# Sparse graph attention with a feed-forward part: records of the second part by GpSimd's queue, mean factors some steps later, gathers asked four groups ahead

## The chip, the cores and the metric

The kernel runs on one core of one Trainium2 chip. The metric is the device time of one launch in microseconds (us), taken as the median of several runs. The core has five engines with a queue each: TensorE (PE in the profile, with its weight loads as PEld), VectorE (DVE), ScalarE (ACT), GpSimd (POOL) and SyncE (SP). An engine works through its queue in order; an instruction that waits holds up all that stand behind it on the same engine. SP, ACT and POOL also issue DMA transfers.

## The reference

The kernel computes one layer of a graph network on 4096 nodes with 512 features and 8 heads of 64:

```python
hs = layer_norm(x);  ht = layer_norm(h_target)
q = (ht @ Wq + bq) / sqrt(64);  k = hs @ Wk + bk;  v = hs @ Wv + bv     # 8 heads
logits = where(adj != 0, q . k, -1e30)          # 4096 x 4096 per head
ctx = softmax(logits) @ v
ht = layer_norm(ht + ctx @ Wo + bo)
ref = ht + gelu(ht @ W1) @ W2                   # 512 -> 2048 -> 512
out = layernorm(x + ref)
```

`adj` is sparse: a random symmetric matrix with a diagonal of ones, so that a target has some 17 neighbours on average and the largest has several tens. All data are float32.

## The kernel before, in words

The kernel does not form the 4096 x 4096 logits. It turns the adjacency matrix into lists of neighbours and gathers the rows of keys and values that each target needs.

**First stage (0 to about 340 us).** It normalises x, computes keys and values (`project`, L882 and on) and writes them to a table `kvd` in DRAM, one row of 1024 numbers per source. At the same time it reads `adj` and extracts the neighbour lists (`edges`) of the first 16 tiles of 128 targets. `sort(0)` orders these targets by their number of neighbours and scatters one record per target (number, target, factors of its first norm, neighbours) into a DRAM array. The lists of the other 16 tiles are built while the second stage already runs, and `sort(1)` scatters their records (L871) at some 800 us. So there are two parts with 16 tiles each, and a tile has 11 to 39 neighbour slots.

**Second stage, attention.** Tiles are taken in an order that pairs long and short ones; pairs are the groups for the feed-forward part. The slots of a tile are worked off in slot groups of three. For each slot, GpSimd issues an indirect DMA (`gather`, L985) that fetches a key and value row for each of the 128 targets into a slot of the ring `kv`. The ring has 17 slots in the first part and 20 in the second. For a slot group VectorE multiplies keys with the query (L1242), reduces to logits (L1247), and, after ScalarE's exponential, multiplies values with the weights (L1203) and adds two of the slots (L1207). ScalarE does the third slot's values (L1226). PE then adds the slots by transposing them into one PSUM tile (`cps`, L1214), after which the ring slots are free. The attention is a Python generator that yields twice per slot group, that is once per half group.

**Records.** `prefetch(i)` (L989 to L999) loads the record of a tile with a small DMA (128 rows of 116 bytes) two tiles before use; six buffers hold them. In the first part GpSimd issues this load, in the second SP.

**Asking for gathers.** `request(k)` (L1060 to L1070) issues the gathers of all slot groups up to `k + ahead`. `ahead` is `AHEAD` = 4, and 5 once slot group k belongs to the second part.

**Finishing a tile.** `finish` (L1097 to L1168) is a generator that is advanced once per half group (`advance`). It scales the context, projects it with Wo, adds the residual into `h`, takes the moments (L697, L698) and, for the last tile of a group, adds EPS (`shifted`, L680), has GpSimd raise it to -0.5 (`power`, L687), multiplies mean and factor on VectorE (`negmean`, L692), lets ScalarE normalise `h` (L1153), and lets PE transpose it to `h2T` (L1162, copied at L1166). The feed-forward part of the group can begin only then.

**Feed-forward.** `feed(g)` takes `h2T` through hidden matmuls (L1347), ScalarE's GELU (L1350) and output matmuls (L1356), in chunks between which it yields. Halfway it has GpSimd gather the rows of x for its targets into `xt`, of which there are two buffers. After its last chunk the generator `end` (L1298 to L1329) adds x (L1303), takes moments, calls `power`, multiplies the mean factor (L1317), normalises on ScalarE (L1320), and has GpSimd scatter the rows to the output (L1324). `end` is advanced once per chunk of the following group.

**What sets the order.** `_weave` interleaves attention, feed-forward, the remaining lists and late weight loads by costs that each generator yields. That gives a program order; a scheduler of the tile framework then orders each engine's queue anew by its own estimates, with program order as the priority. So a step moved in the source shifts instructions on all engines.

Of the kernel before, what the change touches and what calls it, by code (L numbers as in the profile page):

```python
# [17 lines left out]
P = 128  # L18
# [360 lines left out]
RW = E0 + RE  # L379
# [64 lines left out]
def adj_resnorm_kernel(  # L444
# [33 lines left out]
    nc = tc.nc  # L478
# [34 lines left out]
    recs_d = [dram.tile([n * P, RW], I32, name=f"rec{i}") for i, (_, n) in enumerate(PARTS)]  # L513
# [19 lines left out]
    with tc.tile_pool(name="keep", bufs=1) as keep:  # L533
# [17 lines left out]
        with ExitStack() as late:  # L551
# [131 lines left out]
            def power(pool, mv, n, name, ve=None):  # L683
                if ve is None:
                    ve = shifted(pool, mv, n, name)
                rs = pool.tile([P, n], F32, name=name + "_rs")
                nc.gpsimd.tensor_tensor(rs, ve, mhalf[:, :n], ALU.pow)  # L687
                return rs
# [193 lines left out]
            def project(order, t=None):  # L882
# [81 lines left out]
                for n in range(2, 4):  # L964
                    request(n)
# [23 lines left out]
            def prefetch(i):  # L989
                if i >= NT or i in recs:  # L990
                    return
                r0 = TILES[i][0]
                part = 1 if r0 >= PARTS[1][0] * P else 0
                assert part in done
                r0 -= PARTS[part][0] * P
                rec = sp.tile([P, E0 + MAXE], I32, name="rec", bufs=6)

                (nc.sync if part else nc.gpsimd).dma_start(rec[:, :RW], recs_d[part][r0:r0 + P, :])
                recs[i] = rec  # L999

            def front(i, idle=0):
# [28 lines left out]
                for kc in range(KC):  # L1030
# [11 lines left out]
            SG = [(i, j0, min(S, cap - j0)) for i, (_, cap) in enumerate(TILES)  # L1042
                  for j0 in range(0, cap, S)]
# [8 lines left out]
            first_b = next(k for k, (i, _, _) in enumerate(SG) if i >= NA)  # L1052
            issued = [0]
# [6 lines left out]
            def request(k):  # L1060


                ahead = AHEAD + (1 if k >= first_b else 0)
                while issued[0] <= min(k + ahead, len(SG) - 1):
                    issue(issued[0])
                    mine = set(range(place[issued[0]], place[issued[0]] + SG[issued[0]][2]))
                    for m in range(k, issued[0]):
                        assert not mine & set(range(place[m], place[m] + SG[m][2]))
                    issued[0] += 1
# [27 lines left out]
            def finish(i, p, cps, group, hs, mv):  # L1097


                rec, tq, cap = recs[i], tqs.pop(i), TILES[i][1]  # L1100

                nc.vector.scalar_tensor_tensor(p[:, :cap, :], rec[:, E0:E0 + cap].unsqueeze(2)
                                               .to_broadcast([P, cap, H]), 0.0, p[:, :cap, :],
                                               op0=ALU.is_gt, op1=ALU.mult)
                nc.vector.tensor_reduce(sums[:, i, :], p[:, :cap, :].rearrange("p j h -> p h j"),
                                        AX.X, ALU.add)
                ri = sp.tile([P, H], F32, name="ri")
                nc.vector.tensor_scalar_max(ri, sums[:, i, :], SUM_LO)
                nc.vector.reciprocal(ri, ri)
                rx = sp.tile([P, KC, P], F32, name="rb", bufs=1)  # L1110
                rxf = rx.rearrange("p c t -> p (c t)")
                nc.scalar.copy(rxf.rearrange("p (h d) -> p h d", h=H),
                               ri.unsqueeze(2).to_broadcast([P, H, HD]))
                yield
                yield
                prx = ps.tile([P, KC, P], F32, name="t", bufs=2)
                for c in range(KC):
                    nc.tensor.transpose(prx[:, c, :], rxf[:, c * P:(c + 1) * P], ident)
                ct = sp.tile([P, KC, P], F32, name="rb", bufs=1)
                nc.scalar.copy(ct, prx)  # L1120
                yield
                yield
                nc.vector.tensor_mul(ct, cps, ct)
                yield
                yield
                yield
                yield
                pa = ps.tile([P, D], F32, name="t", bufs=2)

                for c in range(KC):  # L1130
                    nc.tensor.matmul(pa[:, c * P:(c + 1) * P], tq[:, D + c * P:D + (c + 1) * P],
                                     ident, is_transpose=True, start=c == 0, stop=False,
                                     skip_group_check=True)
                for c in range(KC):
                    nc.tensor.matmul(pa, ct[:, c, :], wo[:, c, :], start=False,  # L1135
                                     stop=c == KC - 1, skip_group_check=True)
                turned.add(i)
                yield
                h = sp.tile([P, D], F32, name="h")
                nc.scalar.copy(h, pa)  # L1140
                yield
                stats(sp, h, mv[:, len(hs), :], "n2")
                hs.append(h)
                if len(hs) < len(group):
                    return
                nh = len(hs)
                ve = shifted(sp, mv[:, :nh, :], nh, "n2")
                yield
                rs = power(sp, mv[:, :nh, :], nh, "n2", ve)
                yield  # L1150
                nm = negmean(sp, mv[:, :nh, :], rs, nh, "n2")
                for j, h in enumerate(hs):
                    nc.scalar.activation(h, h, AF.Identity, bias=nm[:, j:j + 1], scale=rs[:, j:j + 1])  # L1153
                yield
                yield
                w = len(hs) * P
                h2T = sp.tile([P, KC, 2 * P], F32, name="h2T")
                for k2 in range(KC // 2):
                    pt = ps.tile([P, 2, 2 * P], F32, name="t", bufs=2)
                    for k in range(2):  # L1160
                        for j, h in enumerate(hs):
                            nc.tensor.transpose(pt[:, k, j * P:(j + 1) * P],  # L1162
                                                h[:, (k2 * 2 + k) * P:(k2 * 2 + k + 1) * P], ident)
                    for k in range(2):
                        kc = k2 * 2 + k
                        nc.scalar.activation(h2T[:, kc, :w], pt[:, k, :w], AF.Identity,  # L1166
                                             bias=b2c[:, kc:kc + 1], scale=s2c[:, kc:kc + 1])
                h2Ts[GROUPS.index(group)] = h2T  # L1168
# [129 lines left out]
            def end(group, xs, po):  # L1298

                nt = len(group)  # L1300
                sm = sp.tile([P, 2, 2], F32, name="sm3")
                for j in range(nt):
                    nc.vector.scalar_tensor_tensor(xs[j], xs[j], 1.0, po[j], op0=ALU.mult,  # L1303
                                                   op1=ALU.add, accum_out=sm[:, j, 0:1])
                nc.vector.tensor_scalar_mul(sm[:, :nt, 0], sm[:, :nt, 0], -1.0 / D)
                yield
                for j in range(nt):
                    nc.scalar.activation(po[j], xs[j], AF.Square, bias=sm[:, j, 0:1],
                                         accum_out=sm[:, j, 1:2])
                yield  # L1310
                ve = sp.tile([P, nt], F32, name="n3_ve")
                nc.vector.tensor_scalar(ve, sm[:, :nt, 1], 1.0 / D, EPS, op0=ALU.mult, op1=ALU.add)
                yield
                rs = power(sp, None, nt, "n3", ve)
                yield
                nm = sp.tile([P, nt], F32, name="n3_nm")
                nc.vector.tensor_mul(nm, sm[:, :nt, 0], rs)  # L1317
                yield
                for j in range(nt):
                    nc.scalar.activation(xs[j], xs[j], AF.Identity, bias=nm[:, j:j + 1],  # L1320
                                         scale=rs[:, j:j + 1])
                yield
                for j, i in enumerate(group):
                    ins = nc.gpsimd.indirect_dma_start(  # L1324
                        out=out[:, :], out_offset=bass.IndirectOffsetOnAxis(
                            ap=tags[:, i, TGT:TGT + 1], axis=0),
                        in_=xs[j], in_offset=None)

                    tc.declare_no_dep(ins.ins, group="out", reason="other rows")  # L1329
                    tc.add_to_no_dep_group("out", ins.ins)  # L1330
# [73 lines left out]
            AHEAD = 4  # L1404
# [112 lines left out]
```

## Time and profile before

| what | us |
|---|---|
| median of 3 runs (lowest, highest) | 1804.25 (1801.67, 1813.1) |
| the profiled execution: its own time | 1802.71 |
| its span | 1800.9 |
| PE busy | 1657.8 |
| DVE busy | 1434.2 |
| ACT busy | 1235.6 |
| POOL busy | 1035.2 |

The page gives busy time by engine, groups of instructions by line, engine and tile with the mean duration of one, and the idle time in front of them with the releaser that ended it. Matmuls are pipelined and a matmul of the program can be two records in the trace. An "issue" behind an arrow is time in which the engine waited for nothing that the profile shows. Windows are in us from the start of the span, and the granted clock of TensorE is a share of full speed.

### The profile page before, as it was taken

To read this page: it belongs to the slowest core of one execution; us is meant where nothing else is said; L and a number is where in the kernel's file an instruction comes from. 1 tells how busy PE (TensorE), PEld (TensorE's weight loads), DVE (VectorE), ACT (ScalarE), POOL (GpSimd) and SP (SyncE) were. 2 spreads that over 40 slices of the span, in tenths; PEclk is the share of its full clock that TensorE was granted. 3 is DMA by queue.
4 is the path that set the end of the run, shared out by engine and by line. 5 is a ranking of instruction groups with operands and counts; after the bars stand their busy time and mean duration, and the time that the engine had idled before them with its cause. 6 is when DMAs were issued, how large, how long until landed. Compare 5 with 4: busy or idle time off the path is not lost. (4 is left out here: it accounts for less than half of the span.)

```text
span 1800.9 us, 22314 instructions
## 1 busy us (share of the span) xinstructions
PE 1657.8 (92%) x6746; PEld 1074.4 (60%) x6746; DVE 1434.2 (80%) x2475; ACT 1235.6 (69%) x3129; POOL 1035.2 (57%) x818
## 2 busy tenths in 40 slices
PE   7999995698999999897899989979999999999995
PEld 3444443566666677565566656656666666666663
DVE  6887786889788879988888989789989798998100
ACT  5876663578687967686677877677878587886210
POOL 1000145757555566788777888778777767782100
PEclk9999998799999999998999999989999999999998
DMA  9999978979878787777888888777787767782000
GB/s 350 373 379 361 346 245 306 362 245 317 275 267 284 266 299 256 256 223 221 310 272 267 290 282 270 262 236 259 247 267 245 250 232 235 256 280 95 24 1 26
DMA packets 142058, 460.99 MB, mean 256 GB/s; under 512 B 18548, under 2 KB 23496, under 8 KB 141928
## 3 DMA queue, kind: packets, MB, share of 16 engines
q0 software_dynamic: 96144, 342.27, 56.6%
q1 hardware_dynamic: 37968, 94.12, 14.9%
q10 hardware_dynamic: 7816, 23.08, 3.2%
q8 instruction: 56, 0.92, 0.2%
q14 instruction: 74, 0.61, 0.1%
HBM read 430.61 MB, written 28.79 MB: 255 GB/s over the span
## 5 line engine op out<-in xcount | busy, mean ns | idle before, releaser
L985 POOL DMA_INDIRECT kv<-kvd,rec x603 | 804.5, 1334 | 336.4 <-PE cps L1214 122.5
L1356 PE MATMUL po<-w,gt 128*128 128x512 f32 x1024 | 469.6, 599 | 0.4 <-ACT gt L1350 0.4
L1347 PE MATMUL pf<-h2T,w 128*128 128x256 f32 (+1 forms) x2176 | 467.0, 368 | 0.2 <-ACT h2T L1166 0.2
L1347 PEld LDWEIGHTS pf<-h2T,w 128*128 128x128 f32 x2176 | 389.2, 191 | 68.4 <-issue 23.2
L1226 ACT ACTIVATE kv<-kv,pa 128x64 f32<-128x64 f32 x1520 | 392.1, 337 | 4.8
L1242 DVE TENSOR_TENSOR kv<-kv,tq 128x1536 f32<-128x1536 f32 (+2 forms) x211 | 352.3, 1677 | 48.0 <-DMA kv<-kvd,rec 35.5
L1247 DVE TENSOR_REDUCE lg<-kv 128x24 f32<-128x1536 f32 (+2 forms) x211 | 351.0, 1667 | 0.5
L1214 PE MATMUL cps<-ident,kv 128*128 128x128 f32 x1724 | 241.1, 287 | 76.4 <-DVE kv L1207 38.9
L1356 PEld LDWEIGHTS po<-w,gt 128*128 128x128 f32 x1024 | 189.4, 193 | 191.9 <-issue 189.7
L1214 PEld LDWEIGHTS cps<-ident,kv 128*128 128x128 f32 x1724 | 213.3, 148 | 150.4 <-DVE kv L1207 50.2
L1203 DVE TENSOR_TENSOR kv<-kv,p 128x1024 f32<-128x1024 f32 (+1 forms) x211 | 251.4, 1193 | 10.9 <-ACT p L1251 9.6
L687 POOL TENSOR_TENSOR n_rs<-n_ve,mhalf 128x2 f32<-128x2 f32 (+2 forms) x51 | 51.4, 1007 | 327.5 <-DVE n_ve L680 148.6
L733 ACT ACTIVATE kv<-kv 128x1024 uint8<-128x1024 int32 x128 | 134.4, 1052 | 53.0 <-DMA kv<-in_adj_dram 24.9
L1350 ACT ACT_TABLE_LOAD x108 | 138.6, 1283 | 1.9
L1350 ACT ACTIVATE gt<-pf 128x512 f32<-128x512 f32 x128 | 76.4, 597 | 87.4 <-PE pf L1347 81.8
L947 PE MATMUL pq<-wk,h2T 128*128 128x512 f32 x256 | 121.6, 618 | 4.3 <-ACT kv L949 2.1
L947 PE MATMUL pq<-wv,h2T 128*128 128x512 f32 x256 | 115.6, 594 | 5.8 <-DVE rbc L662 3.2
L1031 PE MATMUL t<-wq,tq 128*128 128x512 f32 x256 | 117.9, 602 | 0.7 <-ACT tq L1024 0.7
L1135 PE MATMUL t<-wo,rb 128*128 128x512 f32 x256 | 115.5, 592 | 0.0
L742 DVE MAX8 cand<-kv 128x8 uint16<-128x171 uint16 (+1 forms) x384 | 108.4, 325 | 6.5 <-remote 3.7
L1251 ACT ACT_TABLE_LOAD x81 | 103.9, 1283 | 1.5
L1207 DVE TENSOR_TENSOR kv<-kv 128x512 f32<-128x512 f32 x144 | 98.2, 682 | 0.2
(163 smaller groups left out, 1501.4 us busy)
## 6 DMA issues: line engine op xcount, KB each, us to landing
kv<-in_adj_dram SPq DMA_DIRECT2D x128, 512.0 KB
kvd<-tq ACTq DMA_DIRECT2D x23, 512.0 KB
kv<-kvd,rec POOLq DMA_INDIRECT x603
kv<-in_L_gnn_h_target_dram SPq DMA_DIRECT2D x32, 256.0 KB
kv<-in_x_dram SPq DMA_DIRECT2D x15, 512.0 KB
kvd<-kv ACTq DMA_DIRECT2D x9, 512.0 KB
w<-in_L_gnn_W_dram SPq DMA_DIRECT2D x4, 1024.0 KB
w<-in_L_gnn_W_dram ACTq DMA_DIRECT2D x4, 1024.0 KB
```

What stands on the lines that cost most here:

```text
L733: nc.scalar.activation(sg, a, AF.Sign, accum_out=dpart[:, i, h:h + 1])
L947: nc.tensor.matmul(pkv, hT[:, kc, j * P:(j + 1) * P], w[:, kc, :], start=kc == 0, stop=kc == KC - 1)
L985: issues[:] = [nc.gpsimd.indirect_dma_start(out=dst, out_offset=None, in_=table[:, :], in_offset=bass.IndirectOffsetOnAxis(ap=idx, axis=0) ...
L1031: nc.tensor.matmul(pq, hT[:, kc, :], wq[:, kc, :], start=kc == 0, stop=kc == KC - 1)
L1203: nc.vector.tensor_tensor(v4, v4, p[:, j0:j0 + m, :].unsqueeze(3) .to_broadcast([P, m, H, HD]), ALU.mult)
L1214: nc.tensor.matmul(cps[:, c, :], kv[:, j, D + c * P:D + (c + 1) * P], ident, is_transpose=True, start=j0 + j == 0 and c == 0, stop=j0 + n ...
L1226: newest[:] = [nc.scalar.mul(v, v, pa[:, hd:hd + 1]).ins]
L1242: nc.vector.tensor_tensor(kv[:, :n, :D], kv[:, :n, :D], tq[:, :D].unsqueeze(1).to_broadcast([P, n, D]), ALU.mult)
L1247: logits[:] = [nc.vector.tensor_reduce(lg[:, :n, :], kv[:, :n, :D].rearrange("p j (h d) -> p j h d", h=H), AX.X, ALU.add).ins]
L1347: nc.tensor.matmul(pf[:, k, :], w1[(f0 + k) // KC][:, kc, (f0 + k) % KC * P:((f0 + k) % KC + 1) * P], h2T[:, kc, :w], start=kc == 0, stop= ...
L1350: nc.scalar.activation(gt, pf, AF.Gelu_apprx_tanh)
L1356: nc.tensor.matmul(po[j], gt[:, k, j * P:(j + 1) * P], w2[(f0 + k) // KC][:, (f0 + k) % KC, :], start=False, stop=f0 + k == FC - 1, skip_g ...
```

## The change

Four edits:

1. All records are loaded by GpSimd's queue, those of the second part too.
2. `request` asks four slot groups ahead in both parts.
3. In `finish`, four steps instead of one lie between the power and the mean factor, so that L692 and the normalisation of `h` behind it come three half groups later in program order.
4. In `end`, one more step lies between the power and the mean factor of the last norm.

```diff
-                (nc.sync if part else nc.gpsimd).dma_start(rec[:, :RW], recs_d[part][r0:r0 + P, :])
+                nc.gpsimd.dma_start(rec[:, :RW], recs_d[part][r0:r0 + P, :])
...
-                ahead = AHEAD + (1 if k >= first_b else 0)
-                while issued[0] <= min(k + ahead, len(SG) - 1):
+                while issued[0] <= min(k + AHEAD, len(SG) - 1):
...
                 rs = power(sp, mv[:, :nh, :], nh, "n2", ve)
-                yield
+                for _ in range(4):
+                    yield
                 nm = negmean(sp, mv[:, :nh, :], rs, nh, "n2")
...
                 rs = power(sp, None, nt, "n3", ve)
                 yield
+                yield
                 nm = sp.tile([P, nt], F32, name="n3_nm")
```

## The prediction

> **What bounds the kernel now.** I read the page first, then the busy time by stage, then the waits of the second stage by engine, then the two places with the longest stalls in order of time.
>
> ```profile
> PE 1657.8 (92%) x6746; PEld 1074.4 (60%) x6746; DVE 1434.2 (80%) x2475; ACT 1235.6 (69%) x3129; POOL 1035.2 (57%) x818
> ```
>
> TensorE is busy for 1657.8 of 1800.9 us and its work is the same in both kernels, so the time can only move with the 143 us in which PE stands still, and with the time in which it runs at half clock after standing still. The stages say where that is (columns: window, length, busy of PE, PEld, DVE, ACT, POOL, granted clock, DMA share, GB/s):
>
> ```profile
> 0.00:340.00 340.00, 286.58 (x803) 141.71 (x804) 261.33 (x908) 209.42 (x430) 85.39 (x97) 0.94 0.94 342
> 340.00:440.00 100.00, 85.74 (x453) 63.40 (x452) 89.12 (x135) 75.53 (x209) 67.79 (x54) 0.93 0.81 287
> 440.00:700.00 260.00, 258.46 (x1177) 179.32 (x1176) 219.45 (x383) 206.40 (x519) 152.96 (x130) 1.00 0.82 279
> 700.00:1210.00 510.00, 462.49 (x1970) 313.01 (x1969) 447.33 (x518) 373.29 (x1023) 396.59 (x297) 0.95 0.79 261
> 1210.00:1650.00 440.00, 435.47 (x1812) 290.75 (x1811) 393.96 (x450) 337.51 (x882) 321.19 (x231) 1.00 0.74 246
> 1650.00:1801.00 151.00, 129.03 (x539) 86.22 (x537) 23.04 (x85) 33.41 (x70) 11.30 (x13) 0.94 0.05 15
> ```
>
> Up to 340 us lies the first stage, which the change doesn't touch. From 440 to 700 and from 1210 to 1650 PE is full. From 700 to 1210 it stands still for 47.5 us. From 1650 on the attention is over and PE works off what is left of the feed-forward part, alone. In 340 to 440 VectorE is at 89 of 100 us and sets the pace.
>
> Who makes PE stand still between 700 and 1650, and what VectorE waits for (engine, instruction, releaser: us, times, longest), in the answers on waits for PE and for DVE:
>
> ```profile
> PE cps L1214 <- DVE kv L1207: 38.9, 12, 11.0
> PE t L1162 <- ACT h L1153: 6.3, 1, 6.3
> ```
> ```profile
> DVE n_nm L692 <- POOL n_rs L687: 36.1, 6, 14.1
> DVE n_nm L692 <- issue: 20.7, 3, 10.8
> DVE n_nm L1317 <- POOL n_rs L687: 8.8, 5, 3.0
> DVE kv L1242 <- DMA kv<-kvd,rec: 8.8, 5, 2.9
> ```
>
> So VectorE loses 56.8 us in front of `negmean` (L692), waiting for GpSimd's power L687, and 8.8 us for gathers. The worst case, in order of time, VectorE and then GpSimd:
>
> ```profile
> 1158.03 0.16 DVE L680 TENSOR_SCALAR n_ve<-mv 128x2 f32<-128x2 f32 x1
> 1158.11 1.75 DVE L1242 TENSOR_TENSOR kv<-kv,tq 128x1536 f32<-128x1536 f32 x1
> 1173.93 0.16 DVE L692 SCALAR_TENSOR_TENSOR n_nm<-mv,n_rs 128x2 f32<-128x2 f32 x1 [14.08 <-POOL n_rs L687]
> ```
> ```profile
> 1163.45 1.01 POOL L1324 DMA_INDIRECT out_dram<-xt,tags  x1 [0.30 <-issue]
> ...
> 1169.70 0.95 POOL L985 DMA_INDIRECT xt<-in_x_dram,tags  x1 [2.71 <-DMA out_dram<-xt,tags]
> ...
> 1173.17 0.73 POOL L687 TENSOR_TENSOR n_rs<-n_ve,mhalf 128x2 f32<-128x2 f32 x1
> ```
>
> The power's input is ready at 1158.2, but GpSimd's queue still has gathers, a scatter of results and an x gather ahead of it, and reaches it 15 us later. VectorE has one multiply (1.75 us) between, then stands for 14.08 us; PE runs dry 8.5 us behind it.
>
> **The change part by part.** The scheduler deals the instructions out again, so I compare the order in which they stand on each engine in the two built programs.
>
> *Mean factor three half groups later.* Nothing is added; L692 moves. What counts is how much VectorE work stands between L680 and L692. For the five stalls between 850 and 1262 us I add up the instructions there, at the durations of their groups on the page (multiply 1.75, reduce 1.74, values 1.22, half add 0.68). Before: 1.9, 3.8, 6.8, 1.9, 1.4 us. After: 5.6, 8.0, 10.9, 8.1, 4.5 us. The power came 6.5, 8.2, 12.7, 15.7 and 3.9 us after L680; with the same lag the stalls of 5.39, 4.85, 6.59, 14.08 and 2.84 us (sum 33.8) leave about 0.9, 0.2, 1.8, 7.6 and 0, and as two or three fewer gathers stand before the power in the fourth and fifth (398 against 400, 436 against 439), 1.3 us each, some 8 us in all: VectorE gets back 26 us. The four later stalls (7.15, 10.77, 4.54 and 0.62 us) keep nearly all of theirs, since there only 0.5 to 2.1 us stand between even after. PE was full around those, so they cost little either way.
> What reaches PE: its gaps right behind the first four stalls are 0.5, 3.0, 6.3 and 8.5 us, 18.3 in all. I let 4 stand (behind the rest of the fourth), so 14 us are gained. Around the two longest the granted clock was 0.66 (1062 to 1072 us) and 0.53 (1173 to 1184 us); PE was busy 5.3 and 6.5 us in these windows, at about half its speed in large part, so 2.5 and 3 us of clock loss go too, and I estimate 1 more behind the 3.0 us gap. Gain 20 us; bounds 8 (another wait takes the place) and 35 (with part of the remaining gaps).
>
> *What is late next: the feed-forward part.* h2T is made from the normalised h, so L1162 moves too: the transposes of `h` stand 8 to 12 value transposes (L1214) further back on PE, and with them the first hidden matmuls. In the order of PE, at its 280th value transpose of 1724 (about 464 us in the trace) 96 hidden and 28 output matmuls (L1347, L1356, two records each) were done before, 80 and 17 after. That lag never closes: at the last value transpose 136 hidden and 60 output matmuls are left before, 152 and 68 after. By the trace 16 records of the hidden kind take 3.62 us and 8 of the output kind 3.60. So 32 records (7.2) and 16 records (7.2) move from about 340 to 440 us, where VectorE sets the pace and PE has 14 idle us already, into the tail, where nothing else runs: +14.4 us. Lower bound +4 (if PE's relief there lets the attention run ahead); upper +18.
>
> *End's norm one step later (an extra step before L1317).* In the new order 15 to 37 us of VectorE work lie between L1312 and the mean factor, so its waits (2.92 us at 808, then 0.6 to 3.0) go. Only the one at 808 lies ahead of a PE gap (11.0 us, ended at 830): gain 3 (0 to 5). The price is that the result scatter L1324 comes later and moves right in front of the next group's x gather, which needs the same buffer: before, 5 to 14 gathers stood between in most groups, after, from the 368th gather on, 0 to 2 in all eight. GpSimd then waits for the scatter to land. In the rows above the scatter ends at 1164.46 and the x gather starts at 1169.70, so a landing takes 5.2 us; less a record load in between about 4 to 4.5 us of hold for each of eight groups, some 35 us of GpSimd.
>
> *Records by GpSimd's queue.* Sixteen issues leave SP and join GpSimd:
>
> ```profile
> L998 POOL DMA_DIRECT2D rec<-rec x16: 537/596/618, 253.1 to 665.6; - x16
> L998 SPq DMA_DIRECT2D rec<-rec x16: 319/320/327, 844.4 to 1417.3; - x16
> ```
>
> 0.60 us each and 0.30 between two issues: 14 us of GpSimd. Behind each stand the gathers, and behind those VectorE's multiply. The Trainium skill's page "DMA: Bandwidth & Descriptors", section "SWDGE vs HWDGE vs iDMA", speaks against this move: plain transfers belong on SP or ScalarE, and what GpSimd issues can be starved of its descriptors while VectorE is in a two-port mode; "SBUF — State Buffer" gives 3.1 us for a transfer that takes 0.62 alone. By that, sixteen would cost up to 50 us of GpSimd. The sixteen of the first part, issued amid the same VectorE work, took 537 to 618 ns, so I use 14. The buffer a record needs (six of them) was freed tiles ago, and it is loaded two tiles before use, so its own landing is covered.
> Does GpSimd's 35 + 14 us reach the end? Between 1000 and 1650 us its gathers wait 55.5 us for ring slots (31.7 for PE, 20.2 and 3.6 for the half adds), and the gathers stand 10 to 16 slots ahead of VectorE's multiply, some four groups of about 6 us. A hold of 4 us is inside that lead; VectorE waited for gathers there only once, 2.0 us. I take 0, the bounds are -2 and +30: the added 49 us nearly use up the 55.5.
>
> *Four groups ahead.* Slots are reused in the order of the ring either way, and the gathers ahead of the powers hardly move (14 and 15 slots ahead before, 10 to 16 after). Value 0, from -4 (shorter queue before a power) to +6 (less lead after a hold).
>
> Sum: 1802.7 (the profiled execution: span 1800.9 and 1.8 around it) + 14.4 - 20 - 3 = 1794.1. The median of the runs is 1.5 us above the profiled one, so 1795.6, say 1795.
>
> **The rivals.**
> *A, forecast:* the stall relief outweighs the feed-forward lag, 1795. Speaks for it: the stall is the longest of VectorE's, and the order puts 3 to 6 us of work into each wait. Chance 0.45.
> *B, all relief reaches the end:* the time from 700 to 1210 us fills up, with the gap at 819 to 830 us and its half clock (11 + 4 us) closed as well: 1804 + 14.4 - 35 - 5 = 1778. Speaks against it: that gap stands where the sixteen list scatters load GpSimd's queue, and they stay. Chance 0.22.
> *C, slower: GpSimd's queue becomes the bound.* The eight holds before the x gathers and the records take 49 us of a slack of 55.5; once holds exceed the lead of four groups (asked four ahead, not five), the multiply L1242 waits for its gathers, PE runs dry and clocks down. It decides from about 6 us a hold, that is if a landing takes 8 us or more. Then half the added GpSimd time shows, 25 us, and half the relief is lost: 1804 + 14.4 - 11 + 25 = 1832; with only some of it, 1820. Speaks for it: single gathers already take up to 5.1 us [...]. Chance 0.25.
> *D, the change doesn't do what it says:* the stalls only move to other instructions that need the power's result, the lag stays: 1804 + 14 - 4 = 1814, inside what counts as no change. Chance 0.08.
>
> **How the numbers follow.** About 1% (18 us) is what a measurement of this kernel can tell from no change, so faster means below 1786, slower above 1822. Faster: most of B and a little of A, 0.27. Slower: most of C, 0.25. Same: 0.48. The range is from 1775 (the relief's upper bound with part of the gap) to 1826 (the lower cases of C). A's own range is 1785 to 1808.
>
> **What would show it.** Right if VectorE's waits at L692 after 700 us fall from 56.8 to about 30 us, PE idles some 30 instead of 47.5 us in 700 to 1210, and the PE-only tail is about 14 us longer. The x gathers should show 30 to 40 us behind the result scatters, without VectorE waiting more than some us for gathers. Wrong if L1242's wait for its gathers grows to tens of us, if PE's gap after 340 us costs more than 18 us, or if the relief at L692 is taken up by another PE wait.

## The result and the profile after

The changed kernel takes 1798.18 us (median of 22 runs, 1792.11 to 1804.37); the kernel before, run beside it, 1805.72 (22 runs, 1795.74 to 1815.32). The ratio is 0.9961, with a 95% interval of 0.9948 to 0.9973: 7 us less. The forecast of 1795 us is 3 us off. That the time is so close to the forecast is luck: two misses of some 10 us each cancel.

The profiled execution after took 1796.99 us, its span 1795.3 (before 1802.71 and 1800.9). From the page, the busy time by engine:

```profile
PE 1660.0 (92%) x6746; PEld 1069.5 (60%) x6746; DVE 1434.3 (80%) x2475; ACT 1238.7 (69%) x3129; POOL 1049.6 (58%) x834
```

TensorE, VectorE and ScalarE do the same work; GpSimd has its 16 record loads more. The stages after (columns as before: window, length, busy of PE, PEld, DVE, ACT, POOL, granted clock, DMA share, GB/s):

```profile
340.00:440.00 100.00, 87.81 (x483) 64.65 (x482) 94.70 (x151) 78.54 (x225) 74.22 (x59) 0.95 0.87 312
700.00:1210.00 510.00, 462.22 (x1983) 311.16 (x1982) 446.86 (x495) 367.69 (x1011) 407.07 (x304) 0.97 0.76 258
1650.00:1796.00 146.00, 132.63 (x544) 88.06 (x542) 20.32 (x84) 35.11 (x70) 15.63 (x17) 0.97 0.07 23
```

From 700 to 1210 us PE stands still for 47.8 us; it was 47.5. The prediction wanted some 30. What VectorE waits for between 700 and 1650 us, and then PE, in the answers on waits after (engine, instruction, releaser: us, times, longest):

```profile
DVE kv L1242 <- DMA kv<-kvd,rec: 33.8, 11, 7.5
DVE tq L1036 <- PE t L1031: 18.6, 5, 6.9
DVE n_nm L692 <- POOL n_rs L687: 17.5, 5, 8.3
DVE kv L1203 <- ACT p L1251: 15.1, 8, 3.7
DVE n_nm L692 <- issue: 7.4, 2, 4.2
DVE tq L1036 <- issue: 6.9, 2, 5.2
```
```profile
PE cps L1214 <- DVE kv L1207: 39.2, 17, 7.4
```

The waits in front of L692 fell from 56.8 to 24.9 us, about as forecast. But VectorE now waits 33.8 us for gathers (before 8.8), 25.5 at L1036 for PE (7.8) and 15.1 at L1203 for the exponential (5.7). PE waits for VectorE's half adds as long as before (38.9).

The longest stall shows how the move itself did its work. VectorE after, in order of time:

```profile
1155.68 0.17 DVE L680 TENSOR_SCALAR n_ve<-mv 128x2 f32<-128x2 f32 x1
...
1166.82 0.16 DVE L692 SCALAR_TENSOR_TENSOR n_nm<-mv,n_rs 128x2 f32<-128x2 f32 x1 [3.17 <-issue]
```

The wait of 14.08 us is one of 3.17. In the window from 795 to 822 us, where the sixteen list scatters are in GpSimd's queue, a new one stands:

```profile
810.56 1.76 DVE L1242 TENSOR_TENSOR kv<-kv,tq 128x1536 f32<-128x1536 f32 x1 [7.52 <-DMA kv<-kvd,rec]
```

Where the 5.6 us of the span come from is read at its end. GpSimd's last scatter of results, before and then after:

```profile
1783.14 1.05 POOL L1324 DMA_INDIRECT out_dram<-xt,tags  x1 [1.38 <-DVE flag L1395]
```
```profile
1786.76 1.04 POOL L1325 DMA_INDIRECT out_dram<-xt,tags  x1 [1.38 <-DVE flag L1396]
```

It comes 3.6 us *later* after, and yet the span ends 5.6 us earlier: 17.8 us lie between it and the end of the span before, 8.5 after. Nothing computes there. The drain that GpSimd runs when its queue is done (number of drains, then shortest, median and longest in ns), before and after:

```profile
L1512 POOLq DRAIN  x3: 44/107/9302, 1790.7 to 1800.6; - x3
```
```profile
L1513 POOLq DRAIN  x3: 44/107/1952, 1792.5 to 1795.0; - x3
```

One drain of 9.30 us has become one of 1.95. Just ahead of the drains stands an instruction that by its name serves the semaphore of GpSimd's own DMAs, before and after:

```profile
L1484 POOLq INC_SWDGE_SEM  x1: 2455/2455/2455, 1788.3 to 1788.3; - x1
```
```profile
L1485 POOLq INC_SWDGE_SEM  x1: 660/660/660, 1791.8 to 1791.8; - x1
```

It fell from 2.46 to 0.66 us. Together that is 9.2 us, more than the whole measured gain of 7. The prediction did not look at this stretch.

### The profile page after: what moved, and what is told of

It reads as the page before. It is cut to its first block, busy times and chain, and to the rows that moved or that the text cites. A ratio compares the mean times of both kernels' runs of the same rounds, so it can differ in the third digit from the quotient of the medians.

```text
span 1795.3 us, 22273 instructions
## 1 busy us (share of the span) xinstructions
PE 1660.0 (92%) x6746; PEld 1069.5 (60%) x6746; DVE 1434.3 (80%) x2475; ACT 1238.7 (69%) x3129; POOL 1049.6 (58%) x834
## 3 DMA queue, kind: packets, MB, share of 16 engines
q0 software_dynamic: 96656, 342.51, 55.8%
## 5 line engine op out<-in xcount | busy, mean ns | idle before, releaser
L985 POOL DMA_INDIRECT kv<-kvd,rec x603 | 817.3, 1355 | 300.7 <-issue 133.2
L1357 PE MATMUL po<-w,gt 128*128 128x512 f32 x1024 | 464.5, 594 | 0.2 <-ACT gt L1351 0.2
L1214 PEld LDWEIGHTS cps<-ident,kv 128*128 128x128 f32 x1724 | 208.5, 146 | 154.1 <-DVE kv L1207 57.1
L1203 DVE TENSOR_TENSOR kv<-kv,p 128x1024 f32<-128x1024 f32 (+1 forms) x211 | 251.7, 1194 | 18.9 <-ACT p L1251 17.7
L1031 PE MATMUL t<-wq,tq 128*128 128x512 f32 x256 | 124.0, 628 | 5.0 <-ACT tq L1024 5.0
L1251 ACT ACTIVATE p<-lg 128x24 f32<-128x24 f32 (+2 forms) x179 | 39.4, 220 | 87.2 <-DVE lg L1247 79.8
```

The lines of the kernel that those rows point to most:

```text
L985: issues[:] = [nc.gpsimd.indirect_dma_start(out=dst, out_offset=None, in_=table[:, :], in_offset=bass.IndirectOffsetOnAxis(ap=idx, axis=0) ...
L1031: nc.tensor.matmul(pq, hT[:, kc, :], wq[:, kc, :], start=kc == 0, stop=kc == KC - 1)
L1203: nc.vector.tensor_tensor(v4, v4, p[:, j0:j0 + m, :].unsqueeze(3) .to_broadcast([P, m, H, HD]), ALU.mult)
L1214: nc.tensor.matmul(cps[:, c, :], kv[:, j, D + c * P:D + (c + 1) * P], ident, is_transpose=True, start=j0 + j == 0 and c == 0, stop=j0 + n ...
L1357: nc.tensor.matmul(po[j], gt[:, k, j * P:(j + 1) * P], w2[(f0 + k) // KC][:, (f0 + k) % KC, :], start=False, stop=f0 + k == FC - 1, skip_g ...
```

## The experiments

Two questions were put. What does each edit do to the body, that is up to the last scatter? And what shortens the drain? Ratios are to runs of the kernel before on the same chip, with 95% intervals. The theories are: the prediction's own (the relief at L692 reaches PE, the later feed-forward part costs up to 14 us); its rival that the wait only moves; and, from the third group of runs on, that the drain decides, set by the number of GpSimd's DMAs, by how late one of them is, or by SP having fewer of its own.

### The mean factor, split in place and done in another way

**Late groups only.** The lag of the feed-forward part arises in the first groups, the long stalls lie in the later ones. So the relief was tried without the lag.

```diff
                 rs = power(sp, mv[:, :nh, :], nh, "n2", ve)
-                yield
+                for _ in range(4 if GROUPS.index(group) >= 6 else 1):
+                    yield
```

> The kernel before, with the mean factor three half groups later only from the seventh feed-forward group on. In the order of PE the feed-forward part then lags 0 us at the 280th value transpose and 3.6 us at the last one, while the VectorE work between L680 and L692 rises to 4.9, 7.8, 10.8 and 3.6 us for the four stalls at 850 to 1174 us. Theory R (the gain is the relief of these stalls, the lag costs 14 us): the relief without its price, ratio about 0.989 to 0.992. Theory L (the lag itself is the gain, since the attention ran 22 us ahead early and the idle time of PE at 700 to 1210 us did not fall): 0.998 to 1.002.

Measured: 0.9997 (0.998 to 1.0015). The waits of VectorE between 700 and 1650 us in this kernel:

```profile
DVE n_nm L692 <- POOL n_rs L687: 43.8, 9, 10.7
DVE kv L1243 <- DMA kv<-kvd,rec: 16.2, 8, 3.3
```

The waits at L692 fell by 13 us only, those for gathers rose by 7, and PE idles 44.6 us from 700 to 1210 (47.5 before). A lag is left, too: from the last value transpose to the last result scatter it is 112.4 us, 108.5 before. A relief of 13 us with 3.9 us of lag comes out at nothing that can be measured.

**Early groups only.** The reverse: `< 6` in place of `>= 6`, the lag without most of the relief.

```diff
-                yield
+                for _ in range(4 if GROUPS.index(group) < 6 else 1):
+                    yield
```

> The kernel before, with the mean factor later only for the first six feed-forward groups. The feed-forward part lags 17 us at the 280th value transpose and 18 at the last, as in the changed kernel, and the VectorE work before the later stalls is 1.2, 3.6, 2.4 and 2.4 us, as before or less. Theory R: the price without the relief, ratio 1.005 to 1.009. Theory L: all of the gain, 0.994 to 0.998.

Measured: 1.0033 (1.0015 to 1.005), 6 us. The waits at L692 are 48.5 us, 56.8 before. The tail from the last value transpose to the last scatter has the whole lag in it, 122.3 us against 108.5. But the attention, relieved of that work of PE, ends 13.1 us earlier (1661.5 against 1674.6), so that less than half of the 14.4 us reaches the time.

**No wait at all for VectorE.** The product goes to GpSimd, behind the power; VectorE only prepares the negated mean, beside L680.

```diff
                 ve = shifted(sp, mv[:, :nh, :], nh, "n2")
+                neg = sp.tile([P, nh], F32, name="n2_neg")
+                nc.vector.tensor_scalar_mul(neg, mv[:, :nh, 0], -1.0)
...
-                nm = negmean(sp, mv[:, :nh, :], rs, nh, "n2")
+                nm = sp.tile([P, nh], F32, name="n2_nm")
+                nc.gpsimd.tensor_tensor(nm, neg, rs, ALU.mult)
```

> The kernel before, with the second norm's mean factor formed on GpSimd right behind the power (VectorE only negates the mean beside L680), so that VectorE never waits at L692; nothing else moves in the order. GpSimd has 17 more small products, about 15 us. Theory R: 56 us of VectorE's waits after 700 us vanish, ratio 0.985 to 0.992. Theory L: VectorE's time comes back as waits for gathers or for PE, 0.997 to 1.003.

Measured: 1.0132 (1.0105 to 1.0159), 24 us slower, which neither theory had, although VectorE has no wait at L692 left. The waits of VectorE in this kernel, and then those of ScalarE, 700 to 1650 us:

```profile
DVE kv L1206 <- ACT p L1254: 42.1, 14, 14.5
```
```profile
ACT h L1156 <- POOL n_nm L1154: 83.5, 10, 15.3
```

ScalarE's normalisation of `h` needs the same power. It stands in ScalarE's queue ahead of exponentials, and ScalarE waits there for 83.5 us (before, at L1153, 64.6: 53.4 for L692 and the rest put down to issue). VectorE then waits for the exponentials behind it: 42.1 us, where it waited 5.7. So the wait before L692 was not VectorE's alone. It held two engines, and setting one free leaves the other held. The prediction's rival "the stalls only move" names this mechanism, to which it gave 0.08, but for the change it does not apply: there the normalisation moves along with L692. Nor is this kernel as clean as it was meant to be. In seven of the ten groups from 700 to 1650 us one to three gathers stand between the power and the product, which then starts up to 9.3 us later, so a part of ScalarE's longer wait is the experiment's own.

**The mean edit alone.** The third edit of the change on the kernel before.

> The kernel before with the mean factor's edit alone, for all groups. Lag 17 and 18 us, VectorE work before the stalls 5.0, 7.8, 10.8, 6.1, 1.9 us. Theory R: relief less lag, about 0.996, most of the whole change. Theory L: the same 0.996. If the records or the four groups ahead carry the change instead: 1.000.

Measured: 1.0087 (1.0058 to 1.0116), 16 us slower. The edit on which the forecast rested makes the kernel slower by itself. Its tail is 122.3 us, as in every kernel with the edit for the early groups or for all.

### The other edits, one alone and one left out

**Four groups ahead alone.** The second edit by itself:

```diff
-                ahead = AHEAD + (1 if k >= first_b else 0)
-                while issued[0] <= min(k + ahead, len(SG) - 1):
+                while issued[0] <= min(k + AHEAD, len(SG) - 1):
```

> The kernel before with four groups asked ahead in both parts, nothing else. The mean factor alone made it 0.9% slower while all four edits make it 0.4% faster, so 1.3% have to come from the other three. Theory A (asking four ahead carries it by itself): ratio about 0.988. Theory I (it helps only together with the later mean factor): 0.998 to 1.002. Theory E (the end's step carries it) : 1.000. In the order, the power of the second norm stands behind up to 3 fewer gathers and the VectorE work before L692 hardly changes (3.6, 2.4, 3.1 us for the stalls at 1052, 1158, 1257 us).

Measured: 1.0061 (1.0045 to 1.0076), 11 us slower.

**All but the mean factor** (edits 1, 2 and 4):

```diff
-                for _ in range(4):
-                    yield
+                yield
                 nm = negmean(sp, mv[:, :nh, :], rs, nh, "n2")
```

> All edits but the later mean factor. Theory A: 0.988. Theory I: 1.000. Theory E: 0.988.

Measured: 0.9994 (0.998 to 1.0009).

**All but the asking ahead** (edits 1, 3 and 4):

```diff
-                while issued[0] <= min(k + AHEAD, len(SG) - 1):
+                ahead = AHEAD + (1 if k >= first_b else 0)
+                while issued[0] <= min(k + ahead, len(SG) - 1):
```

> All edits but the four groups ahead (five again in the second part). Theory A and theory I: as the mean factor alone, 1.007 to 1.011. Theory E: 0.996. VectorE work before L692 at the stalls from 1158 us on: 6.2, 0.8, 0.0, 0.0 us, against 8.0, 4.3, 1.9, 0.3 in the changed kernel.

Measured: 1.0095 (1.0063 to 1.0128).

**All but the step in `end`** (edits 1, 2 and 3):

```diff
                 rs = power(sp, None, nt, "n3", ve)
                 yield
-                yield
```

> All edits but the end's extra step. Theory A and theory I: as the changed kernel, 0.995 to 0.998. Theory E: 1.007 to 1.011.

Measured: 0.9961 (0.9943 to 0.998), the same as the whole change. The fourth edit does nothing that can be measured. Of the theories, I met the last three results and comes nearest; none had that four groups ahead alone would cost 11 us.

To read these together, the program's end has to be taken out. Kernels with edit 1 have the short end, which is 9.2 us or 0.51% of 1800 us. With it added back, what the body does is in the third column (0.13 to 0.33% to either side). The last two columns are counted in the traces by the work and not by the clock: the time from the 1200th of the 1724 value transposes to the last, and from the last to the last result scatter.

| edits | ratio | body alone | 1200th to last transpose, us | to the last scatter, us |
|---|---|---|---|---|
| none (before) | 1 | 0 | 551.8 | 108.5 |
| mean (3) | 1.0087 | +0.87% | 562.5 | 122.3 |
| mean without ahead (1, 3, 4) | 1.0095 | +1.46% | 566.4 | 122.3 |
| ahead (2) | 1.0061 | +0.61% | 561.6 | 108.5 |
| ahead without mean (1, 2, 4) | 0.9994 | +0.45% | 567.9 | 108.5 |
| both (1, 2, 3) | 0.9961 | +0.12% | 546.1 | 122.3 |
| both (the whole change) | 0.9961 | +0.12% | 544.6 | 122.3 |

Without the other, each of the two edits costs 0.45 to 1.46%; together they cost nothing that can be told from zero. The fourth column shows a stretch where this comes about: 10 to 16 us lost with one of them, 6 to 7 gained with both. Windows from 1190 to 1680 us of before, after, the mean edit alone and four groups ahead alone (the third number is PE's busy time):

```profile
1190.00:1680.00 490.00, 481.88 (x1998) 323.70 (x1998) 425.48 (x529) 368.79 (x962) 335.53 (x242) 0.99 0.70 230
```
```profile
1190.00:1680.00 490.00, 484.16 (x1992) 320.46 (x1991) 415.90 (x521) 367.07 (x944) 327.50 (x249) 1.00 0.68 230
```
```profile
1190.00:1680.00 490.00, 474.21 (x1954) 316.23 (x1953) 410.08 (x510) 346.08 (x913) 333.73 (x237) 0.99 0.68 226
```
```profile
1190.00:1680.00 490.00, 472.48 (x1945) 312.44 (x1944) 417.31 (x480) 360.02 (x950) 326.37 (x241) 0.99 0.70 231
```

PE stands still for 8.1 us before and 5.8 after, but 15.8 with the mean edit alone and 17.5 with four groups ahead alone. The two kernels with one of them left out stand still for 18.3 us (all but the mean) and 17.4 (all but ahead). The kernel with all but ahead stands still longer between 700 and 1210 us as well (61.2 against 47.5 us). The cause within the stretch is not settled. With four groups ahead and without the mean edit, VectorE waits 25.1 and 33.9 us between 700 and 1650 us for PE at L1036 (7.8 before, 18.6 after). With the mean edit and without four groups ahead, PE waits for ScalarE's copies of `h2T` (7.3 and 7.9 us in front of L1021), and VectorE for gathers (38.1 and 37.4 us, but with both edits, too, it is 33.8 and 37.2). Since the scheduler deals out every queue anew after each edit, one wait can't be singled out by edits of this kind. It stays open.

### The program's end

**Records alone.** The first edit by itself:

```diff
-                (nc.sync if part else nc.gpsimd).dma_start(rec[:, :RW], recs_d[part][r0:r0 + P, :])
+                nc.gpsimd.dma_start(rec[:, :RW], recs_d[part][r0:r0 + P, :])
```

> The kernel before with all records by GpSimd's queue and nothing else; the order on the other engines stays. In all profiles so far with this edit the program ends 7.5 to 7.7 us after the last result scatter was issued, in all without it 16.4 to 16.9 us: the drain at GpSimd's end takes about 2 instead of 9.3 us. Theory T (this edit gives a fixed 9 us at the end, whatever stands before): tail 7.5 us, ratio about 0.995. Theory Q (sixteen more issues on GpSimd cost it 14 us where it has no slack): 1.000 to 1.005.

Measured: 0.9958 (0.9942 to 0.9974), as much as the whole change. In this kernel VectorE's waits at L692 are 53.5 us, so none of the relief is in it. GpSimd's drain:

```profile
L1512 POOLq DRAIN  x3: 44/107/1952, 1787.7 to 1790.2; - x3
```

**One record.** Only the load of the last tile moves from SP to GpSimd.

```diff
-                (nc.sync if part else nc.gpsimd).dma_start(rec[:, :RW], recs_d[part][r0:r0 + P, :])
+                (nc.sync if part and i + 1 < NT else nc.gpsimd).dma_start(rec[:, :RW], recs_d[part][r0:r0 + P, :])
```

> The kernel before with only the record of the very last tile loaded by GpSimd, the other fifteen of the second part by SP. If the short end comes from how lately GpSimd has last issued a plain DMA (theory T1), tail 7.5 us and ratio 0.995. If it comes from the number of issues by GpSimd or by SP (theory T2), tail 16.5 us and ratio 1.000.

Measured: 0.9931 (0.9904 to 0.9958), 1787.4 us against 1798.37. This is the fastest kernel of the study. It beats the kernel before; against the change, whose interval (0.9948 to 0.9973) it overlaps a little, it lies lower by 0.3%. Its drain is the shortest:

```profile
L1512 POOLq DRAIN  x3: 44/107/727, 1788.6 to 1789.9; - x3
```

The semaphore instruction ahead of it takes 0.36 us. From the last scatter to the end of the span it is 6.0 us, 11.8 less than before. The scatter itself comes 1.5 us later behind the last value transpose (110.0 us against 108.5), so some 10.4 us are left; that is 0.58% of 1798 us, and 0.69% (0.42 to 0.96) was measured. One load added to GpSimd's 749 DMAs does all of this, and it is issued at 1428 us, some 360 us ahead of the drain.

**Late groups' mean factor with the records.**

```diff
-                (nc.sync if part else nc.gpsimd).dma_start(rec[:, :RW], recs_d[part][r0:r0 + P, :])
+                nc.gpsimd.dma_start(rec[:, :RW], recs_d[part][r0:r0 + P, :])
...
-                yield
+                for _ in range(4 if GROUPS.index(group) >= 6 else 1):
+                    yield
```

> The later mean factor only from the seventh group on, which alone gave 0.9997, and all records by GpSimd. Theory T: the product, about 0.994 to 0.995, a little faster than all four edits (0.996).

Measured: 0.9961 (0.994 to 0.9981), the same as records alone: once more nothing that can be measured from the late relief and its 3.9 us of lag together.

**Sixteen more loads early on.** Is it the number of GpSimd's DMAs, or a late one, or SP's smaller number? Each record of the first part is loaded a second time by GpSimd, into a tile that nothing reads. SP keeps its sixteen records, and GpSimd's last loads are where they were.

```diff
                 recs[i] = rec
+                if not part:
+                    scr = sp.tile([P, RW], I32, name="scr", bufs=1)
+                    nc.gpsimd.dma_start(scr, recs_d[part][r0:r0 + P, :])
```

> The kernel before, records of the second part by SP as before, but each of the first part's sixteen records is loaded a second time by GpSimd into a tile that nothing reads. GpSimd so issues 765 DMAs, as many as with all records, none of them late and SP's sixteen stay. In the profiles the last drain on GpSimd took 9.30 us with 749 issues by GpSimd, 0.73 with 750 and 1.95 with 765. If the number alone sets it (theory N): drain 1.95 us, program's end 7.5 us after the last scatter, ratio 0.995 to 0.997. If it matters that a record of the second part comes by GpSimd or that SP's are fewer (theory S): drain 9.3 us, end 16.7 us, ratio 1.000 to 1.002.

Measured: 1.002 (0.9998 to 1.0043). The drain, and the waits of GpSimd up to 400 us, in this kernel:

```profile
L1515 POOLq DRAIN  x3: 44/107/1952, 1803.0 to 1805.5; - x3
```
```profile
POOL scr L1002: 27.2, 12
```

The drain is 1.95 us, with 765 DMAs as in the whole change, so neither a late load nor fewer by SP is needed for the short drain; the number is enough. The time missed its expectation, because the edit brings a wait of its own: the added loads share one buffer, each waits for the one before to land (27.2 us of GpSimd), and the first value transpose starts at 308.0 instead of 296.1 us.

GpSimd issues 749 DMAs before: 603 gathers of keys and values, 32 each of x rows, targets, list scatters and result scatters, 16 records and 2 others. The whole series:

| GpSimd's DMAs | kernels | longest drain, us | last scatter to the end, us |
|---|---|---|---|
| 749 | before, and five that leave the records on SP | 9.30 | 17.4 to 18.0 |
| 750 | one record | 0.73 | 6.0 |
| 765 | the change, five parts or mixtures with all records on GpSimd, sixteen more loads | 1.95 | 8.4 to 8.8 |

All fourteen profiles fit it. What in the number decides is not shown: the drain does not grow with it, only three numbers were seen, and the packets of GpSimd's queue go along with it (96144, 96176 and 96656).

## Why the prediction was right, and where it was wrong

**"14 us are gained" behind the stalls, 20 with the clock: the waits went, but only a part reached the time, and here the prediction failed.** VectorE got back 31.9 us at L692, 26 were forecast, and the 14.08 us stall shrank to 3.17. ScalarE, whose normalisation of `h` stands behind L692 and moved with it, was freed as well: at L1153 it waits 22.5 us where it waited 64.6. Before, then after (what is left is put down to issue):

```profile
ACT h L1153 <- DVE n_nm L692: 53.4, 8, 13.3
```
```profile
ACT h L1153 <- DVE n_nm L692: 12.4, 5, 4.7
```

And PE's gaps behind the stalls did close: those of 3.0, 6.3 and 8.5 us are now 1.7, 0.9 and none. PE before, then after:

```profile
968.20 1.81 PE L1214 MATMUL cps<-ident,kv 128*128 128x128 f32 x8 [3.03 <-DVE kv L1207]
1066.73 0.69 PE L1162 MATMUL t<-ident,h 128*128 128x128 f32 x2 [6.28 <-ACT h L1153]
1177.54 1.97 PE L1214 MATMUL cps<-ident,kv 128*128 128x128 f32 x8 [8.46 <-DVE kv L1207]
```
```profile
964.14 1.09 PE L1214 MATMUL cps<-ident,kv 128*128 128x128 f32 x8 [1.72 <-DVE kv L1207]
1072.33 0.44 PE L1162 MATMUL t<-ident,h 128*128 128x128 f32 x2 [0.88 <-ACT h L1153]
```

That is 15.2 us, where 14 were forecast. What the step left out is that PE would stand still elsewhere instead. After, between 790 and 1040 us, these gaps are new, or longer (the second was 4.03):

```profile
794.36 6.16 PE L1031 MATMUL t<-wq,tq 128*128 128x512 f32 x8 [4.56 <-ACT tq L1024]
872.81 1.97 PE L1214 MATMUL cps<-ident,kv 128*128 128x128 f32 x8 [6.80 <-DVE kv L1207]
908.92 1.97 PE L1214 MATMUL cps<-ident,kv 128*128 128x128 f32 x8 [3.47 <-DVE lg L1247]
992.45 1.09 PE L1214 MATMUL cps<-ident,kv 128*128 128x128 f32 x8 [3.20 <-DVE kv L1207]
1034.13 1.31 PE L1214 MATMUL cps<-ident,kv 128*128 128x128 f32 x8 [4.04 <-DVE kv L1207]
```

So PE's idle time from 700 to 1210 is 47.8 us against 47.5, though the granted clock there rose from 0.95 to 0.97. The stretch from the 800th to the 1200th value transpose takes 311.5 us against 311.7, and only the one behind it, to the last, is shorter: 544.6 against 551.8. Why the new gaps opened is not shown. VectorE waits longer for gathers (+25.0 us), at L1036 (+17.7) and at L1203 (+9.4); that these are the price of the relief is argued, not shown.

**"+14.4 us" for the feed-forward part: right in the tail, to the size.** From the last value transpose to the start of the last output matmul it is 103.8 us before and 117.5 after, 13.7 us longer:

```profile
L1214 PE MATMUL cps<-ident,kv x28: 272/273/328, 1643.0 to 1664.5; 128*128 128x128 f32 x28
L1357 PE MATMUL po<-w,gt x144: 592/592/697, 1656.4 to 1782.0; 128*128 128x512 f32 x144
```

(From 1640 us for the first line and 1650 for the second.) But the attention ended earlier, 1664.5 against 1674.6 us. Of these 10.1 us 3.5 were there at the first value transpose (292.6 against 296.1 us), before the change does anything; the first stage of single profiles differs by some us. The step held that between 340 and 440 us VectorE sets the pace, so that what PE leaves out there is lost. It was not so: at the 280th value transpose the changed kernel is 22 us ahead (442 against 464 us; 3 us of that were there at the 80th), and VectorE is busy for 94.7 of the 100 us, where it was 89.1. PE's order held the attention back, and an engine that is busy for 89 of 100 us was not yet the bound. Later the lead goes again, to 3 us at the 800th; why is open. With most of the relief left out the lag cost 6 us (1.0033), inside the prediction's bounds, whose lower one, +4, names just this: PE's relief lets the attention run ahead.

**"Gain 3" for `end`'s step: 0.** Its waits went (10.2 us at L1317 before, none after), and all but this step has the same ratio as all. The x gathers wait for result scatters for 17.7 us, 13 times (8.1 us, 7 times, before), where some 35 were forecast. The mechanism was right and the hold about 1.4 us each, not 4.

**"Records: I take 0": right in the body, and this step missed the largest term.** The sixteen loads cost what the first part's rows said:

```profile
L998 POOL DMA_DIRECT2D rec<-rec x32: 537/601/632, 250.0 to 1416.4; - x32
```

The 3.1 us that the Trainium skill gives in "SBUF — State Buffer", section "A bandwidth-pool intuition that's wrong (but worth ruling out)", for a transfer that GpSimd issues beside a VectorE copy did not appear: these loads took 0.63 us at the longest. Whether VectorE was then in the mode that the skill names, no run here shows. With the records alone the ratio is 0.9958, and the shorter end, 9.2 us or 0.51%, is inside what that interval allows. The bound of "-2" below left no room for it: the prediction counted each DMA by its issue, its landing and who waits for it, and not what the queue does when the program ends, though the trace of before shows the 9.30 us drain.

**"Value 0, from -4 to +6" for four groups ahead: this step failed.** Alone it costs 11 us (1.0061), and with the mean edit in place it gains: 1.0095 without it and 0.9961 with it, 1.3%. The prediction costed each edit as if it stood alone and added the sums. Here the edits don't add.

The sum, then, was 14.4 - 20 - 3 = -8.6 us in the body and 0 at the end. Measured are 7 us less in all (2.3 us to either side by the interval). The traces put -9.2 of them at the end and +13.8 in the tail, which leaves about -11.6 for the attention, where -23 were forecast. So the gain in the attention came out at half its size, and the missing 11 us were made up by 9 us at the end that the prediction did not have: range and sign held by luck. Rival C's sign came, since gathers kept VectorE waiting for 33.8 us instead of 8.8, but not its mechanism. Those waits go with the mean edit (30.8 to 38.1 us in the five kernels with it for the early groups or for all, 4.4 to 20.2 in the others) and not with the records (12.6 with the records alone), and the time did not rise to what C had forecast.

## What to carry to other kernels

Before a wait is moved, look for every engine that waits for the same producer: freeing one of them leaves the others held. When gaps have closed, look for where the engine stands still instead, and measure stretches by the work done in them and not by the clock. Work that is put off is paid at the end, but what it left free may be gained before. Price edits that let a scheduler deal the order anew as a set, since two that lose alone can cancel each other. And read the trace past the last instruction that computes: here as much as the whole gain lay in a drain that belongs to no line of the algorithm, and a single DMA moved to another queue was worth more than all of the reordering.

## What the hardware showed unexpectedly

With 749 DMAs issued by GpSimd, that semaphore instruction and GpSimd's longest drain took 2.46 and 9.30 us at the program's end; with 750 they took 0.36 and 0.73, with 765 0.66 and 1.95. With 765 it did not matter for the length whether the sixteen added loads were issued early (251 to 382 us) or late (in the change up to 1416 us), nor whether SP had issued sixteen fewer. The lengths go in steps: 0.73 us and 1 or 7 times 1.225 us make the three drains, 0.36 us and 1 or 7 times 0.30 us the three semaphore instructions. So both seem to count the same thing, which no run here names. Why 749 and 750 differ so much isn't explained by any run here.
